# Projection of a windowless attention block: weights loaded once, the constant product earlier, more room for the attention's output

## The chip, the cores and the metric

One core of one Trainium2 chip runs the whole kernel. The metric is device time in microseconds, from one launch; the number quoted is the median over runs. The profile shows one execution of it. Units in the text are microseconds from the start of the profiled span unless another unit is named.

## The reference, cut to what matters

The input x is 2 images of 48 x 48 tokens with 768 channels, in float32. Layer 0 is attention over all 2304 tokens of an image, with 12 heads of 64 channels and a relative position term by row and by column; layer 1 mixes channels in the Fourier domain. What the change touches is the end of layer 0:

```python
x = x + attention(_gn(x))          # layer 0
    # attn = softmax(q k^T * scale + rel_h + rel_w)
    # out  = (attn @ v)  -> (B, 48, 48, 768)
    # return out @ proj_w + proj_b
x = x + fourier_mix(_gn(x))        # layer 1
```

`proj_w` is 768 x 768, which is 2.36 MB.

## The kernel before, in words

The two images run one after the other. For each, `attention` walks over 108 **units**: 6 pairs of heads, 6 groups g of 8 image rows, 3 parts x. Unit n is number 0 to 107 of an image. A unit has 128 queries, 2 heads and all 2304 keys, and goes through these steps:

- POOL writes the position terms of the unit into a tile `s` (`new_unit`, one 128 x 2304 operation for each head). There are three buffers of `s`.
- TensorE makes the scores by pieces of 512 keys (`ps_s`), DVE adds them to `s` and keeps the maxima (`mx`, then `nm`).
- ACT makes the exponentials in place (`numerators`).
- DVE transposes 32 x 32 blocks (`squares`, in two halves), and `exchange` moves the blocks between partitions into `pT`: 3 of 4 by DMAs from SP's queue, the fourth by ACT. When the second half has left, the buffer of `s` is free again.
- TensorE multiplies by the values (`weigh`, tile `ps_o`, two units later), ACT copies the result to `res`, and at each third unit SP sends it to `oT` in DRAM. The sums of exponentials are inverted, turned by TensorE (`ps_i`) and sent to `inv_d` in DRAM, for three groups at a time (`inverses`, with `turn` and `send`).

While a pair is weighed, the keys, values and queries of the next are made, so TensorE has work between the units. The last pair has no next one.

In the loop over n, one step is: scores of n, exponentials, work ahead, then what `late` fills in, then weighing of n - 2, then the second half of the exchange of n - 1, the first half of n, `finish`, the next `new_unit`, and the next step of `late`. Most instructions of `attention` and `Projection` are issued through `InOrder`, so that they keep the written order on their engine; others (`new_unit`, the bias addition, the loads of constants) may be put elsewhere by the scheduler. Line 68 is the helper that records all `InOrder` operations, so groups there are told apart by their tiles. A DMA from SP uses one of eight completion lanes in turn and waits for the one that used the lane before it.

`Projection` (line 571 on) lives in the large buffer `span`, which held the normalised input `xnT` during attention: the weights `w`, the bias `pb`, two buffers of a group of attention output `o_sb` (384 tokens, 768 channels) and one of the inverses `inv`, both read back from DRAM by `parts` and multiplied by POOL (`proj<-proj` in the profile). Its steps are run at the ends of units 102 to 108:

| unit | SP and POOL (`step`) |
|---|---|
| 102, 103, 104 | two sixths of `proj_w` each |
| 105 | half of group 0 of `oT`, `proj_b` |
| 106 | other half, first half of `inv` |
| 107 | second half of `inv`, POOL's multiplication |
| 108 | all of group 1 |

The bias of the values, times `proj_w`, is a constant row (`values_bias`, tile `ps_pb`): it is made once, in image 1, added to `pb` by DVE (line 638), and kept in DRAM as `pb_d` for image 2. `product(t, hf)` makes a 128-token, 384-channel piece of the projection (tile `acc`, 6 matmuls, 36 pieces in an image). `late(n - len(order) + 2)` puts some of this TensorE work in front of the last weighings: in image 1 half of the constant product before weighing 105, the other half and one piece before 106, three pieces before 107; in image 2 two pieces before 106 and three before 107.

`project_out` then loops over 18 tiles of 128 tokens: it loads rows of x into `x2` (`rows`), POOL adds `pb`, TensorE makes the remaining pieces, DVE adds each to its rows of `x2` (line 742), and finished rows go through the first Fourier matrix (`ps_y`, `over_w`) to DRAM. PSUM has seven rotating banks for all of this and one for `ps_o`.

Of the kernel before, what the change touches and what calls it, by code (L numbers as in the profile page):

```python
# [9 lines left out]
F32 = mybir.dt.float32  # L10
# [150 lines left out]


def attention(tc, k, x_b, a, oT, inv_d, late, span, ps_b, ps_o):

# [8 lines left out]
    with ExitStack() as ctx:  # L176
# [319 lines left out]
        for n in range(len(order) + 3):  # L496
            un = older = None
            if n < len(order):
                un = ahead
                pr, g, x = order[n]  # L500
                if g == 4 and x == 0 and pr + 1 < NP:
                    weights[0] = load_w(0, pr + 1)
                scores(un)
                recent.append(un)
            write = read = None
            if un is not None:
                numerators(un)
                ready, staged = staged, None
                if x == 2:
                    if n + 4 < len(order):  # L510
                        key = order[n + 4][:2]
                        staged = (key, queries(*key))
                    if g == 2 and pr + 1 < NP:
                        weights[2] = load_w(2, pr + 1)
                    if g == 5 and pr + 2 < NP:
                        weights[1] = load_w(1, pr + 2)
                elif n < 2:
                    for i in range(3):
                        values(0, 3 * n + i)
                    if n:  # L520
                        weights[1] = load_w(1, 1)
                elif pr + 1 < NP:
                    i = 2 * g + x
                    for j in range(0 if n == 3 else i, i + 1):
                        (keys if j < 6 else values)(pr + 1, j % 6)
                if ready is not None:
                    key, qT = ready
                    rhw, write, read = relative(key[1], qT)
                    groups[key] = (qT, rhw)
            if turn is not None:  # L530
                turn()
                turn = None
            if n >= len(order) - 1 and recent:
                late(n - len(order) + 2)
            if n > 1 and recent:
                older = recent.pop(0)
                weigh(older)
            evict(by_act)
            if last is not None:
                squares(last, 1)  # L540
                exchange(last, 1)
            if write is not None:
                write()
            if un is not None:
                squares(un, 0)
                exchange(un, 0)
            evict(by_dve)
            if read is not None:
                read()
            if older is not None:  # L550
                finish(older)
            if un is not None and n + 1 < len(order):
                ahead = new_unit(*order[n + 1])
            if send is not None:
                send()
                send = None
            if older is not None and older["x"] == 2 and older["g"] % 3 == 2:
                turn, send = inverses(older["pr"], older["g"] // 3)
            if len(order) - 6 <= n <= len(order):
                late()  # L560
            last = un


# [12 lines left out]
class Projection:  # L576


    def __init__(self, tc, k, a, oT, inv_d, span, ps_b, dram):
        self.nc = nc = tc.nc  # L580
        self.k, self.a, self.ps_b, self.dram = k, a, ps_b, dram
        self.oT_v = oT.rearrange("(cc p) s -> p cc s", p=P)
        self.inv_d = inv_d
        self.whole = span.tile([P, NCC * S], F32, tag="span", name="proj")
        self.w = self.whole[:, : NCC * C].rearrange("p (cc f) -> p cc f", f=C)
        self.pb = self.whole[:, NCC * C : (NCC + 1) * C]
        self.o = {}
        self.pe, self.sync, self.pool = (
            InOrder(tc, e) for e in (nc.tensor, nc.sync, nc.gpsimd)
        )  # L590
        w_v = a["proj_w"].rearrange("(cc p) f -> p cc f", p=P)
        load = lambda cc: nc.sync.dma_start(out=self.w[:, cc], in_=w_v[:, cc])
        parts = iter(self.parts(0))
        self.steps = [
            lambda: (load(0), load(1)),
            lambda: (load(2), load(3)),
            lambda: (load(4), load(5)),
            lambda: (next(parts), self.bias()),
            lambda: next(parts),
            lambda: list(parts),  # L600
            lambda: self.tokens(1),
        ]
        self.accs, self.waiting, self.late = {}, [], 1
        if k.pb_d is None:
            self.late = 0
            self.waiting += [lambda hf=hf: self.values_bias(hf) for hf in range(2)]
        for t in range(3):
            self.waiting += [lambda t=t, hf=hf: self.product(t, hf) for hf in range(2)]

    def step(self):  # L610
        self.steps.pop(0)()

    def fill(self, n):

        for _ in range(n - self.late):
            self.waiting.pop(0)()
        self.late = 0

    def bias(self):

# [3 lines left out]
    def values_bias(self, hf):  # L624


        nc, k = self.nc, self.k
        cols = slice(hf * UQ, (hf + 1) * UQ)
        ps = self.ps_b.tile([P, 512], F32, tag="b", name="ps_pb")
        for cc in range(NCC):  # L630
            self.pe.matmul(
                ps[:, :UQ],
                lhsT=k.bv[:, cc : cc + 1].to_broadcast([P, P]),
                rhs=self.w[:, cc, cols],
                start=(cc == 0),
                stop=(cc == NCC - 1),
            )
        nc.vector.tensor_tensor(self.pb[:, cols], ps[:, :UQ], self.pb[:, cols], ALU.add)
        if hf:
            k.pb_d = self.dram.tile([C], F32, tag="pb_d", name="pb_d")  # L640
            nc.sync.dma_start(out=k.pb_d, in_=self.pb[0, :])

    def product(self, t, hf):

        if (t, hf) not in self.accs:
            o_sb = self.o[t // 3]
            acc = self.ps_b.tile([P, 512], F32, tag="b", name="acc")
            for cc in range(NCC):
                self.pe.matmul(
                    acc[:, :UQ],  # L650
                    lhsT=o_sb[:, cc, (t % 3) * P : (t % 3 + 1) * P],
                    rhs=self.w[:, cc, hf * UQ : (hf + 1) * UQ],
                    start=(cc == 0),
                    stop=(cc == NCC - 1),
                )
            self.accs[t, hf] = acc
        return self.accs[t, hf]
# [5 lines left out]

    def parts(self, g):

        at = [(NCC + 1) * C + i * NCC * UQ for i in range(3)]
        o_sb, inv = (
            self.whole[:, c0 : c0 + NCC * UQ].rearrange("p (cc s) -> p cc s", s=UQ)
            for c0 in (at[g % 2], at[2])
        )  # L670
        for h in range(2):
            cc = slice(h * NCC // 2, (h + 1) * NCC // 2)
            self.sync.dma_start(out=o_sb[:, cc], in_=self.oT_v[:, cc, g * UQ : (g + 1) * UQ])
            if h == 0:
                yield
        for h in range(2):
            self.sync.dma_start(
                out=inv[h * HD : (h + 1) * HD],
                in_=self.inv_d[:, g // 3, h, g % 3, :].partition_broadcast(HD),
            )  # L680
            if h == 0:
                yield
        self.pool.tensor_tensor(o_sb, o_sb, inv, ALU.mult)
        self.o[g] = o_sb
        yield


def project_out(tc, k, x_b, pr, pools, y_d, x2, constants):
# [366 lines left out]
def block_kernel(tc, a, out):  # L1055
    nc = tc.nc
    B = a["x"].shape[0]
    with ExitStack() as ctx:
# [11 lines left out]
        nc.gpsimd.memset(k.eps, GN_EPS)  # L1070
        k.load(nc, a, cp, {"rel": [P, 2 * REL]})
        k.pb_d = None
        k.bv = cp.tile([P, NCC], F32, tag="bv", name="bv")
        with nc.allow_non_contiguous_dma(reason="biases onto partitions"):
            nc.sync.dma_start(
# [3 lines left out]
        for b in range(B):  # L1079
            oT = dram.tile([C, S], F32, tag=f"oT{b}", name=f"oT{b}")  # L1080
            y_d = dram.tile([YP, HW // 2, C], F32, tag=f"y_d{b}", name=f"y_d{b}")
            inv_d = dram.tile([NP, 2, 2, 3, UQ], F32, tag=f"inv_d{b}", name=f"inv_d{b}")
            ready = []

            def late(fill=0):
                if not ready:
                    ready.append(Projection(tc, k, a, oT, inv_d, span, ps_b, dram))
                if fill:
                    ready[0].fill(fill)
                else:  # L1090
                    ready[0].step()

            attention(tc, k, a["x"][b], a, oT, inv_d, late, span, ps_b, ps_o)
            with ExitStack() as ctx2:
                pool = lambda name, bufs, **kw: ctx2.enter_context(
# [9 lines left out]
                with ExitStack() as ctx3:  # L1105
                    work = ctx3.enter_context(tc.tile_pool(name="po_w", bufs=2))
                    project_out(
                        tc, k, a["x"][b], ready[0], (ps_b, work), y_d, x2, constants
                    )
                u_pool, w_pool, z_pool = pool("sp_u", 6), pool("sp_w", 2), pool("sp_z", 1)  # L1110
                y_pool = pool("sp_y", 8)
# [100 lines left out]
```

## Time and profile before

| | |
|---|---|
| median of 3 runs | 3811.16 us (3810.2 to 3815.46) |
| the profiled execution | 3818.63 us |
| its span, first to last instruction | 3816.8 us |
| mean granted TensorE clock | 0.978 |
| TensorE busy (PE) | 3660.0 us, 96% |
| DVE, ACT, POOL busy | 2845.0, 2516.4, 1993.1 us |
| DMA | 607.00 MB, 67.4% of 16 engines on SP's queue |
| handover from attention to projection, image 1 | about 1390 to 1500 us |
| the same, image 2 | about 3294 to 3400 us |

In a timeline, each row is the start, the duration, the engine, the line, the operation with output <- input, the shape, the count of instructions merged, and in brackets the idle time before it with what ended it. SPq rows are issues of DMAs, not their transfers. In a table of stretches a stretch is start:end, its length, and the busy time of PE, PEld, DVE, ACT and POOL with counts, then the granted clock, the DMA share and the rate. A float32 matmul is two rows for TensorE.

### The profile page before, as it was taken

The numbers are of one execution on the slowest core, as the hardware profiler recorded it, in microseconds if no ns is written. First come the engines' busy times: TensorE is split into PE (matmuls) and PEld (weight loads), VectorE is DVE, ScalarE is ACT, GpSimd is POOL, SyncE is SP. The second block draws the span as 40 slices with busy tenths as digits, with TensorE's granted clock in tenths as the row PEclk, the third lists the DMA queues.
The fourth block names the chain that finished last, engine by engine and source line by source line (L and its number), as shares of the span: only waits on it lengthen the run. The fifth ranks groups of instructions, "written<-read, shape, count | busy, mean of one in ns | idle before, by whom it ended". The sixth has DMA issues, their size and how long they took to land.

```text
span 3816.8 us, 83418 instructions
## 1 busy us (share of the span) xinstructions
PE 3660.0 (96%) x31520; PEld 2596.1 (68%) x31520; DVE 2845.0 (75%) x6692; ACT 2516.4 (66%) x3690; POOL 1993.1 (52%) x598
## 2 busy tenths in 40 slices
PE   8999999999999887999989999999999999879999
PEld 6677776767777665566666777777677776645665
DVE  4788888888888883335557988889888898833445
ACT  3688888888888882133237888888888888821331
POOL 2466666666666664412125666666666666633121
PEclk9999999999999998999989999999999999989899
DMA  3677777777777887633526777777777778885334
GB/s 103 144 176 167 174 170 170 173 163 178 166 176 166 171 190 184 165 101 110 167 81 143 172 173 168 177 165 174 164 177 166 173 171 170 194 189 151 103 103 134
DMA packets 497821, 607.00 MB, mean 159 GB/s; under 512 B 180493, under 2 KB 312973, under 8 KB 497422
## 3 DMA queue, kind: packets, MB, share of 16 engines
q1 hardware_dynamic: 497422, 601.69, 67.4%
q8 instruction: 250, 4.10, 0.5%
q14 instruction: 149, 1.22, 0.1%
HBM read 131.61 MB, written 87.67 MB: 57 GB/s over the span
## 4 chain that ended last, share of the span: by engine, by line
PE 84%; DMA 5%; DVE 4%; POOL 3%; SPq 2%; issue 1%; ACT 1%; POOLq 0%; DVEq 0%; ACTq 0%
PE ps_o L68 20%; PE ps_s L68 19%; PE ps_proj L68 14%; PE ps_v L68 8%; PE acc L68 7%; PE ps L948 4%; DVE s L68 3%; POOL s L344 3%; DMA pT<-s 2%; PE ps_z L892 2%; PE ps L920 2%; PE ps L924 2%; PE ps_u L983 2%; SPq L68 2%; PE ps_y L721 2%; PE ps_r L68 1%
## 5 line engine op out<-in xcount | busy, mean ns | idle before, releaser
L344 POOL TENSOR_TENSOR s<-rhw 128x2304 f32<-128x2304 f32 x432 | 1744.8, 4060 | 1144.6 <-DMA pT<-s 601.1
L68 DVE CUSTOM_DVE_ANT_0 s<-ps_s,s 128x512 f32<-128x512 f32 (+1 forms) x2160 | 1223.6, 633 | 371.7 <-issue 243.3
L68 ACT ACTIVATE s<-s,nm 128x1152 f32<-128x1152 f32 x864 | 1074.7, 1245 | 452.5 <-DVE nm L68 414.8
L68 DVE STREAM_TRANSPOSE s<-s 128x1152 f32<-128x1152 f32 x864 | 1111.8, 1344 | 5.5 <-ACT s L68 5.5
L68 ACT COPY pT<-s 32x1152 f32<-32x1152 f32 x864 | 993.2, 1150 | 19.5 <-DVE s L68 2.1
L68 PE MATMUL ps_o<-pT,v 128*64 128x128 f32 x15552 | 919.7, 278 | 47.9 <-DMA pT<-s 21.8
L68 PEld LDWEIGHTS ps_o<-pT,v 128*64 128x64 f32 x15552 | 867.8, 140 | 112.2 <-issue 53.8
L68 PE MATMUL ps_s<-kT,qT 64*128 64x512 f32 (+1 forms) x4320 | 918.5, 558 | 13.4 <-DVE mx L68 9.8
L68 PEld LDWEIGHTS ps_s<-kT,qT 64*128 64x128 f32 x4320 | 431.4, 186 | 450.7 <-issue 333.9
L68 PE MATMUL ps_proj<-xnT,w 128*128 128x384 f32 (+1 forms) x2016 | 597.0, 450 | 2.3 <-ACT gn_rstd L151 2.3
L68 PEld LDWEIGHTS ps_proj<-xnT,w 128*128 128x128 f32 x2016 | 360.8, 191 | 209.0 <-DVE mx L68 41.0
L68 PE MATMUL acc<-proj 128*128 128x384 f32 x864 | 287.5, 492 | 40.5 <-POOL proj L68 40.5
L742 DVE TENSOR_TENSOR x<-acc,x 32x384 f32<-32x384 f32 (+2 forms) x216 | 119.2, 553 | 277.3 <-PE acc L68 192.6
L68 PEld LDWEIGHTS ps_v<-w,xnT 128*128 128x128 f32 x2592 | 295.9, 193 | 21.2 <-DVE mx L68 21.2
L68 PE MATMUL ps_v<-w,xnT 128*128 128x128 f32 x2592 | 308.1, 279 | 0.0
L965 POOL TENSOR_TENSOR spectrum<-spectrum 128x480 f32<-128x480 f32 x80 | 96.3, 1204 | 345.0 <-DVE spectrum L964 186.6
L68 PEld LDWEIGHTS acc<-proj 128*128 128x128 f32 x864 | 165.8, 193 | 156.6 <-POOL proj L68 41.3
L728 ACT COPY y<-ps_y 112x384 f32<-112x384 f32 x96 | 45.9, 478 | 265.8 <-PE ps_y L721 248.7
L68 DVE DVE_READ_ACCUMULATOR2_ANT mx<- 128x1 f32 x2160 | 178.9, 83 | 0.0
L68 POOL TENSOR_TENSOR proj<-proj 128x2304 f32<-128x2304 f32 x12 | 60.6, 5052 | 197.5 <-DMA proj<-inv_d 169.7
L68 ACT ACTIVATION_READ_ACCUMULATOR s<-s,nm 128x1 f32 x864 | 161.1, 186 | 0.0
L928 ACT ACTIVATE spectrum<-ps,b 96x400 f32<-96x400 f32 x96 | 56.6, 589 | 147.7 <-PE ps L924 147.7
(97 smaller groups left out, 2099.6 us busy)
## 6 DMA issues: line engine op xcount, KB each, us to landing
pT<-s SPq DMA_DIRECT2D x2592, 144.0 KB
t<-rel SPq DMA_DIRECT2D x144, 189.0 KB
rhw<-t SPq DMA_DIRECT2D x144, 144.0 KB
y<-y_d SPq DMA_DIRECT2D x40, 360.0 KB
u_d<-spectrum SPq DMA_DIRECT2D x40, 360.0 KB
u<-u_d SPq DMA_DIRECT2D x48, 300.0 KB
xt<-in_x SPq DMA_DIRECT2D x12, 1152.0 KB
w<-in_qkv_w SPq DMA_DIRECT2D x36, 384.0 KB
```

What stands on the lines that cost most here:

```text
L68: return lambda *args, **kw: self.tc.keep_in_program_order(op(*args, **kw))
L344: nc.gpsimd.tensor_tensor(s[:, h, :].rearrange("p (y x) -> p y x", x=HW), rhw[:, x, h, :HW][:, :, None].to_broadcast([P, HW, HW]), rhw[:, ...
L721: nc.tensor.matmul(ps[:YP, : 2 * SC], lhsT=k.fw, rhs=part[:, t0 : t0 + 2, ch], start=True, stop=True,)
L728: nc.scalar.copy(y1[:, :, ch], ps[:YP, : 2 * SC].rearrange("p (t c) -> p t c", c=SC))
L742: nc.vector.tensor_tensor(dst, acc[p : p + n, :UQ], dst, ALU.add)
L892: nc.tensor.matmul(ps[:BS, w * 96 : (w + 1) * 96], lhsT=self.y2[s, j][:, w, i * BS : (i + 1) * BS], rhs=k.fh, start=True, stop=True,)
L920: nc.tensor.matmul(ps[:BS, :400], lhsT=w1[:, wa, i, :], rhs=zf[:, 0, fs], start=True, stop=False,)
L924: nc.tensor.matmul(ps[:BS, :400], lhsT=w1[:, wb, i, :], rhs=zf[:, 1, fs], start=False, stop=True,)
L928: nc.scalar.activation(self.o1[:, ri, fs], ps[:BS, :400], AF.Gelu, bias=self.b1[:, n, ri : ri + 1])
L948: nc.tensor.matmul(ps[64 * r : 64 * r + 64, w * BS : (w + 1) * BS], lhsT=self.o1[:, ri, f0 : f0 + 64], rhs=w2[:, (0, 2, 1, 0)[2 * r + ri], ...
L965: nc.gpsimd.tensor_tensor(val, val, clip, ALU.subtract)
L983: nc.tensor.matmul(ps[: 2 * HW, :480], lhsT=k.ih, rhs=d2[:, c0 : c0 + 480], start=True, stop=True)
```

## The change

- **Weights once.** `proj_w` gets a tile of its own (`k.w`, 18 KB in each partition) for the whole kernel, loaded by one DMA at the end of unit 3 of image 1 and used for both images.
- **Constant product in the last pair.** `values_bias` is filled in by the iterations of units 103 and 104 instead of 107 and 108.
- **Room.** The space that the weights leave in `span` is given to a third buffer of `o_sb` and a second one of `inv`.
- **Earlier first group.** The steps of group 0 run at units 102, 103 and 104, with the bias at 102; units 105 to 107 have empty steps; group 1 stays at 108. The products ahead are 1, 2 and 3 pieces before the weighings 105, 106 and 107, in both images.
- The closure `late` becomes the class `Late`, and a scratch size for dynamic DMAs is set to 1024.

```diff
-            if n >= len(order) - 1 and recent:
-                late(n - len(order) + 2)
+            if n >= len(order) - 6 and recent:
+                late.fill()
...
+            if n == 3:
+                late.weights()
             if len(order) - 6 <= n <= len(order):
-                late()
+                late.step()
...
-        self.w = self.whole[:, : NCC * C].rearrange("p (cc f) -> p cc f", f=C)
-        self.pb = self.whole[:, NCC * C : (NCC + 1) * C]
+        self.pb = self.whole[:, :C]
...
-        load = lambda cc: nc.sync.dma_start(out=self.w[:, cc], in_=w_v[:, cc])
-        parts = iter(self.parts(0))
+        parts = self.parts(0)
         self.steps = [
-            lambda: (load(0), load(1)),
-            lambda: (load(2), load(3)),
-            lambda: (load(4), load(5)),
             lambda: (next(parts), self.bias()),
             lambda: next(parts),
-            lambda: list(parts),
+            lambda: next(parts),
+            lambda: None,
+            lambda: None,
+            lambda: None,
             lambda: self.tokens(1),
         ]
...
+        bias = [lambda hf=hf: self.values_bias(hf) for hf in range(2)] if k.pb_d is None else []
+        early = [
+            lambda t=t, hf=hf: self.product(t, hf) for t in range(3) for hf in range(2)
+        ]
+        self.waiting = [[], bias[:1], bias[1:], [], [], early[:1], early[1:3], early[3:]]
...
-        at = [(NCC + 1) * C + i * NCC * UQ for i in range(3)]
+        at = [C + i * NCC * UQ for i in range(5)]
...
-            for c0 in (at[g % 2], at[2])
+            for c0 in (at[g % 3], at[3 + g % 2])
...
+class Late:
...
+    def weights(self):
+
+        if not self.k.w_there:
+            self.k.w_there = True
+            self.sync.dma_start(
+                out=self.k.w, in_=self.a["proj_w"].rearrange("(cc p) f -> p cc f", p=P)
+            )
...
+        k.w = cp.tile([P, NCC, C], F32, tag="w", name="w")
...
-    nc = bacc.Bacc("TRN2", target_bir_lowering=False, num_devices=1)
+    nc = bacc.Bacc("TRN2", target_bir_lowering=False, num_devices=1, dynamic_dma_scratch_size=1024)
```

More of the change, by code (lines that the diff above doesn't have):

```diff
@@ L590, in __init__, with fill @@
         )
-        w_v = a["proj_w"].rearrange("(cc p) f -> p cc f", p=P)
-        load = lambda cc: nc.sync.dma_start(out=self.w[:, cc], in_=w_v[:, cc])
-        parts = iter(self.parts(0))
+        parts = self.parts(0)
         self.steps = [
-            lambda: (load(0), load(1)),
-            lambda: (load(2), load(3)),
-            lambda: (load(4), load(5)),
             lambda: (next(parts), self.bias()),
             lambda: next(parts),
-            lambda: list(parts),
+            lambda: next(parts),
+            lambda: None,
+            lambda: None,
+            lambda: None,
             lambda: self.tokens(1),
         ]
[L603 to L608, printed above, removed]
+        bias = [lambda hf=hf: self.values_bias(hf) for hf in range(2)] if k.pb_d is None else []
[3 more added lines that the diff above has]
+        self.waiting = [[], bias[:1], bias[1:], [], [], early[:1], early[1:3], early[3:]]
+        self.accs = {}
     def step(self):
         self.steps.pop(0)()
[L613 to L617, printed above, removed]
+    def fill(self):
+        for issue in self.waiting.pop(0):
+            issue()
     def bias(self):
@@ L633, in values_bias @@
                 lhsT=k.bv[:, cc : cc + 1].to_broadcast([P, P]),
-                rhs=self.w[:, cc, cols],
+                rhs=k.w[:, cc, cols],
                 start=(cc == 0),
@@ L651, in product @@
                     lhsT=o_sb[:, cc, (t % 3) * P : (t % 3 + 1) * P],
[L652 removed]
+                    rhs=self.k.w[:, cc, hf * UQ : (hf + 1) * UQ],
                     start=(cc == 0),
@@ L685, in parts, with __init__, fill, step @@
         yield
+class Late:
+    def __init__(self, tc, k, a, *rest):
+        self.k, self.a, self.made = k, a, None
+        self.make = lambda: Projection(tc, k, a, *rest)
+        self.sync = InOrder(tc, tc.nc.sync)
+    def weights(self):
[4 more added lines that the diff above has]
+            )
+    def fill(self):
+        self.made = self.made or self.make()
+        self.made.fill()
+    def step(self):
+        self.made = self.made or self.make()
+        self.made.step()
 def project_out(tc, k, x_b, pr, pools, y_d, x2, constants):
@@ L1072, in block_kernel @@
         k.pb_d = None
+        k.w = cp.tile([P, NCC, C], F32, tag="w", name="w")
+        k.w_there = False
         k.bv = cp.tile([P, NCC], F32, tag="bv", name="bv")
@@ L1082, in block_kernel @@
             inv_d = dram.tile([NP, 2, 2, 3, UQ], F32, tag=f"inv_d{b}", name=f"inv_d{b}")
[L1083 to L1091, printed above, removed]
+            late = Late(tc, k, a, oT, inv_d, span, ps_b, dram)
             attention(tc, k, a["x"][b], a, oT, inv_d, late, span, ps_b, ps_o)
@@ L1107, in block_kernel @@
                     project_out(
-                        tc, k, a["x"][b], ready[0], (ps_b, work), y_d, x2, constants
+                        tc, k, a["x"][b], late.made, (ps_b, work), y_d, x2, constants
                     )
```

## The prediction

> **What bounds the kernel now.** I read the granted clock first (0.978 in the one profiled execution), then busy time by stretch, then engine by engine the timeline where attention hands over to the projection, because every edit acts there. Over most of attention TensorE is never idle (300.00 us busy of 300.00 between 600 and 900 us), so nothing there pays but less TensorE work, and the change has exactly as many matmuls as before. At the handover it is otherwise. By stretch (PE, PEld, DVE, ACT, POOL, then clock, DMA share, GB/s):
>
> ```profile
> 300.00:600.00 300.00, 300.00 (x2790) 217.23 (x2791) 264.91 (x631) 250.58 (x346) 192.08 (x48) 1.00 0.76 170
> 1390.00:1430.00 40.00, 31.69 (x286) 23.96 (x288) 31.50 (x75) 30.77 (x41) 24.00 (x7) 0.83 0.99 225
> 1430.00:1470.00 40.00, 21.39 (x183) 14.04 (x179) 22.36 (x49) 22.15 (x28) 12.12 (x3) 0.81 0.94 219
> ```
>
> The last six units of image 1 fill the DMA engines and leave TensorE idle for a quarter to half of the time. TensorE's timeline shows where the long gap is:
>
> ```profile
> 1433.56 3.70 PE L68 MATMUL ps_s<-kT,qT 64*128 64x512 f32 x14
> 1440.04 4.14 PE L68 MATMUL ps_pb<-proj,bv 128*128 128x384 f32 x12
> 1444.10 4.15 PE L68 MATMUL ps_o<-pT,v 128*64 128x128 f32 x72
> 1448.18 4.14 PE L68 MATMUL ps_pb<-proj,bv 128*128 128x384 f32 x12
> 1470.60 6.50 PE L68 MATMUL acc<-proj 128*128 128x384 f32 x12 [18.28 <-POOL proj L68]
> 1481.11 11.88 PE L68 MATMUL acc<-proj 128*128 128x384 f32 x36
> 1497.12 15.65 PE L68 MATMUL acc<-proj 128*128 128x384 f32 x48
> ```
>
> The last scores end at 1440.1 (T). The first product waits 18.28 us for POOL's multiplication of group 0. After 1497 TensorE runs without a gap to 1644: the projection is TensorE-bound. A product is 12 of these rows (each matmul is two) and takes 15.48/4 = 3.87 us at full clock. The queue, POOL and DVE rows that the steps need:
>
> ```profile
> 1393.49 1.01 SPq L592 DMA_DIRECT2D proj<-in_proj_w  x2
> 1471.91 0.61 SPq L68 DMA_DIRECT2D x<-in_x  x1
> 1497.41 0.35 SPq L68 DMA_DIRECT2D oT<-res  x1
> 1497.86 2.38 SPq L68 DMA_DIRECT2D inv_d<-turned  x3
> 1405.55 8.07 POOL L344 TENSOR_TENSOR s<-rhw 128x2304 f32<-128x2304 f32 x2 [8.13 <-DMA pT<-s]
> 1418.37 8.07 POOL L344 TENSOR_TENSOR s<-rhw 128x2304 f32<-128x2304 f32 x2 [4.75 <-DVE mx L68]
> 1429.56 8.08 POOL L344 TENSOR_TENSOR s<-rhw 128x2304 f32<-128x2304 f32 x2 [3.11 <-DMA pT<-s]
> 1465.51 5.03 POOL L68 TENSOR_TENSOR proj<-proj 128x2304 f32<-128x2304 f32 x1 [27.88 <-DMA pT<-s]
> 1390.95 5.15 DVE L68 STREAM_TRANSPOSE s<-s 128x1152 f32<-128x1152 f32 x4
> 1399.22 0.69 DVE L68 CUSTOM_DVE_ANT_0 s<-ps_s,s 128x512 f32<-128x512 f32 x1 [3.08 <-issue]
> ```
>
> **1. What is gained: the wait for group 0, and more products under attention.** Before, from T to TensorE's steady stretch: image 1, 1497.3 - 1440.1 = 57.2 us with 4 of 36 products done, 32 left; image 2 (scores end 3341.6, steady at 3399.8) 58.2 us with 31 left; there the same gap is 22.2 us. After, group 0 is multiplied before the last unit's scores, so TensorE runs from T on: 1 product, weighing 105, 2 products, weighing 106, 3 products, weighing 107: 6 x 3.87 + 3 x 4.1 = 35.5 us. Call its end W = T + 35.5. The exchange of unit 107 does not hold it: before, its last DMA was issued 22.7 us after T.
>
> **2. What is late next: the rows of x.** In the built order of the changed kernel, SP's `x<-in_x` no longer stands before `oT<-res` and the three `inv_d<-turned` of the last unit, but behind them. Before it was issued 25 us ahead of `oT<-res`; now it can only follow weighing 107: by the rows above, 0.34 us to `oT<-res`, 0.45 to the first and 2.4 for the three `inv_d`, so W + 3.3. Six accumulators hold six of seven PSUM banks until DVE adds them to rows of x. The seventh, freed when the small transpose of the inverses is copied, takes one more product (the first of group 1, which POOL has multiplied by about W: loads issued near T + 18, 13 us to land, 5.03), and then TensorE stops. Landing: between 6 and 21 us the 1.18 MB loads of x run at 398 to 411 GB/s, and the first, issued at 1.67, lets TensorE start at 8.21: 6.5 us; in image 2 before, the same load took 13.3 us (issued 3371.64, POOL starts on it at 3384.98), but behind 2.4 MB of group 1. Now the queue ahead is empty, so I take 6, with 5 and 13.3 as ends. Then two rows of POOL (1.8 us each) and DVE's adds (0.55): 4.3. TensorE resumes at W + 3.3 + 6 + 4.3 = W + 13.6; after the gap of 9 us it runs slowly (6.50 us for the first product after the 18 us gap, against 3.87), so I add 2: W + 15.6, with 29 products left.
>
> The Trainium skill (TensorE: Matmul & The Clock Gate, Part 1) says that an idle window of about 3.4 us halves TensorE's clock until about 3.4 us of work have passed. It speaks against trading one gap for another: by it the new gap would cost up to 1.7 us of lost work, against the 2 taken from the row. The trace agrees with the halving: the granted clock is 0.50 from 1456 to 1474.
>
> From T: 35.5 + 15.6 = 51.1 us. Image 1: 57.2 - 51.1 + 3 x 3.87 = **17.7** gained; image 2: 58.2 - 51.1 + 2 x 3.87 = **14.8**. Later groups do not wait: group 2's load is issued by about W + 10 and took 13.5 us before (1503.1 to 1516.6), and is needed near W + 40. The third buffer therefore gains nothing by itself; it was not waited for before (TensorE had no gap there).
>
> **3. What moves T: image 1.** `proj_b` is now loaded at unit 102, in the place of the first weights (1393.49), behind half of group 0 (0.59 MB). DVE's first addition of the constant product stands, in the built order, between unit 103's maxima (1390.87) and the transposes at 1390.95, and must wait for that load. Queued behind it on DVE are these transposes; for them wait the exchange DMAs, POOL (three buffers of s in a ring) and the next scores. Ahead of the load the reads of rhw land at 1398.8 (chain of waits), then 0.98 MB at 225 to 400 GB/s: about 1402.3. Ends: 1396 (the stall is then 5 us, of which 3 were idle anyway) and 1408 (13.3 us after issue, as the x row). So the transposes start near 1402.9, unit 104's scores at 1408 instead of 1399.2 (+9). Around the ring: POOL gets unit 102's buffer 7 us after its transposes end, at 1412.5 instead of 1405.55, unit 105's scores end 8.5 late, and unit 106's 7 late, since part is made up in the 4 to 8 us that POOL idled between tiles. Then comes POOL's multiplication of group 0 (5.03 us), which the built order puts between units 106 and 107: 1434 to 1439, unit 107's tile until 1447 instead of 1437.6. Unit 107's scores end near 1452 instead of 1443.1: T is **8.9** late. The 2.36 MB of weights that go from this stage don't relieve it at once: 2.75 MB of groups and bias are now in units 102 to 104 and not in 105 to 107. The constant product itself (2 x 4.14) fits into gaps of 2.9 and 3.5 us that TensorE had there: nothing, or 1 us each where it doesn't fit.
>
> **4. What moves T: image 2.** No constant product. Units 102 and 103 load 0.98 and 1.18 MB instead of 0.79 each, and of smaller pieces: at the 215 GB/s of group loads against 400 of weights, +1.7 and +3.5 us for the buffers that POOL waits for; unit 106's scores end 3.5 late. The multiplication then takes POOL from 3332.1 to 3337.2 and unit 107's tile ends at 3345.3 instead of 3338.8; the scores, 5.1 us of which need it, end at 3350.4 instead of 3344.5: T is **5.9** late. Ends of this: 2.9 (POOL's 5.03 less its 2.2 us idle) and 8.
>
> **5. The weights' single load.** 2.36 MB after unit 3's reads of rhw (149.85), where SP was idle until 153.78. At 405 GB/s it is 5.8 us, at 225 10.5. TensorE has no gap there, so a delay is lost: the next exchange lands 1.5 to 6 us late, against 1 us of margin at unit 6's scores. I take **1**, ends 0 and 5. The Fourier constants, now behind x, land by W + 10 and are first used near W + 20; the second layer's tables are first used 150 us later: nothing.
>
> **Sum.** 17.7 + 14.8 - 8.9 - 5.9 - 1 = 16.7 us gained. The profiled execution took 3818.63 us (span 3816.8 and 1.8 around it), 7.5 above the median of the runs, 3811.16. The same difference from the median gives **3794 us**; a profile would show a span near 3800.
>
> By the skill's page on DMA (DMA: Bandwidth & Descriptors, Anatomy of one DMA), a load takes 2 us and bytes at 436 GB/s: an estimate of 4.7 us for x against the 6 taken, and 7.4 us for the weights; with it the sum would be 2.6 us better.
>
> **Rivals.**
> *The stalls are hidden* (0.12). If `proj_b` lands by 1396, T in image 1 is late by POOL's multiplication alone, 3 us, and a sum of 22 to 26 remains: 3785 to 3789. For it: unit 104's scores had 3 us to spare. Against: a DMA share of 0.99 at that place.
> *Late landings, slower* (0.14). Every load that the change puts on the path lands as the slowest near row, 13.3 us after issue: x in both images (+14.6), the bias (+5.7 in image 1), group 0's divisors at POOL (+2): 16.7 - 22.3, so 3817. It decides from landings of about 11.5 us. For it: group loads took 13.5; against: the queue is empty at W. If only x is late, 3809, which is no change (0.12).
> *It doesn't do what it says*: excluded, since the built order has one load of the weights, at unit 3, and six products ahead.
>
> **How the numbers follow.** Forecast 0.62 (its own range 3783 to 3803). About 0.2%, or 7.6 us, is what a measurement of this kernel can tell from no change. Faster: forecast and hidden stalls, less a little, 0.72; same 0.14; slower 0.14. Range 3780 to 3813: hidden stalls with a quick x below, half of the slower rival above.
>
> **What would show it.** Right: no 18 us gap before the first product; a gap of about 9 us one product after weighing 107, ended by DVE's adds to x; DVE idle about 11 us before the addition in image 1 only; POOL's multiplication between units 106 and 107. Wrong: if x lands before W, if unit 107's scores end as early as before, or if units 4 to 7 of image 1 show TensorE gaps over 5 us.

## The result and the profile after

The changed kernel took **3810.81 us** (median of 12 runs, 3803.2 to 3817.08) beside 3812.27 us for the kernel before (12 runs); the ratio is 0.9994, 95% interval 0.9985 to 1.0003. A second group of runs gave 3812.57 us (11) beside 3816.48 us (27), again 0.9994 (0.9985 to 1.0002). So the change makes no difference that can be measured. The forecast was 16.7 us faster, so it was wrong, although 3811 lies inside the stated range.

Every event that the prediction named can be seen in the profile. First the stretches of the last six units (PE, PEld, DVE, ACT, POOL, clock, DMA share, GB/s):

```profile
1390.00:1430.00 40.00, 30.21 (x226) 19.47 (x226) 26.60 (x67) 23.54 (x31) 17.99 (x5) 0.85 0.79 185
1430.00:1470.00 40.00, 37.69 (x324) 26.58 (x322) 28.79 (x62) 30.91 (x41) 19.30 (x5) 0.94 0.83 174
```

The DMA share has fallen from 0.99 and 0.94, and the second stretch, which held the 18.28 us gap, is nearly full. But TensorE is no busier in the first (30.21 us against 31.69), and later comes a new gap. TensorE's timeline of image 1:

```profile
1403.32 1.27 PE L68 MATMUL ps_s<-kT,qT 64*128 64x512 f32 x2 [2.72 <-DVE proj L635]
1409.04 2.93 PE L68 MATMUL ps_s<-kT,qT 64*128 64x512 f32 x6 [4.44 <-DVE mx L68]
...
1451.40 4.11 PE L68 MATMUL acc<-w,proj 128*128 128x384 f32 x12
...
1488.10 4.11 PE L68 MATMUL acc<-w,proj 128*128 128x384 f32 x12 [0.39 <-issue]
1502.65 6.06 PE L68 MATMUL acc<-w,proj 128*128 128x384 f32 x12 [10.45 <-DVE x L764]
```

The products run ahead from T = 1451.4 without a wait for group 0. One product after weighing 107 TensorE stops for 10.45 us, and then the first product takes 6.06 us. The two gaps on top, in unit 104's scores, stand behind VectorE, whose addition to `proj_b` waits for the load of `proj_b` and holds up what is queued behind it. VectorE's, SyncE's and POOL's timelines at these places:

```profile
1402.71 0.56 DVE L635 TENSOR_TENSOR proj<-ps_pb,proj 128x384 f32<-128x384 f32 x1 [10.15 <-DMA proj<-in_proj_b]
```

```profile
1487.84 0.34 SPq L68 DMA_DIRECT2D oT<-res  x1
1488.27 2.37 SPq L68 DMA_DIRECT2D inv_d<-turned  x3
1490.69 0.45 SPq L68 DMA_DIRECT2D x<-in_x  x1
```

```profile
1436.19 5.08 POOL L68 TENSOR_TENSOR proj<-proj 128x2304 f32<-128x2304 f32 x1
1441.22 8.08 POOL L343 TENSOR_TENSOR s<-rhw 128x2304 f32<-128x2304 f32 x2
...
1498.45 14.14 POOL L68 TENSOR_TENSOR x<-x,proj 96x768 f32<-96x768 f32 x8 [11.41 <-DMA x<-in_x]
```

VectorE stood for 10.15 us before the addition. The rows of x are issued 3.26 us after weighing 107 (1487.43) and reach POOL 7.76 us later. Image 2 has the same gap, and there the first early product is slow too; POOL, SyncE and TensorE of image 2:

```profile
3386.48 0.45 SPq L68 DMA_DIRECT2D x<-in_x  x1
...
3394.41 14.15 POOL L68 TENSOR_TENSOR x<-x,proj 96x768 f32<-96x768 f32 x8 [13.94 <-DMA x<-in_x]
```

```profile
3344.55 6.71 PE L68 MATMUL acc<-w,proj 128*128 128x384 f32 x12
...
3398.62 6.98 PE L68 MATMUL acc<-w,proj 128*128 128x384 f32 x12 [10.66 <-DVE x L764]
```

A difference of a few us in the whole can't be read from one execution of each kernel: the spectral layer takes 253.6 to 259.3 us in image 1 (up to the norm of image 2) and 258.5 to 264.2 us in image 2 from one profile to the next, though none of the edits touches its lines. From R to Z the two profiles of the changed kernel agree within 1.3 us for each stage. So I read the account by stages of TensorE's timeline. u8: start of unit 8's scores; R: end of the last `ps_r`, a small product behind the position terms (in unit 102); T: end of the last scores; W: end of the last weighing (the start of the row behind it); Z: first `ps_z` of the spectral layer. The columns are times between these points in us.

```
                      image 1                              image 2
             0-u8    u8-R     R-T    T-W     W-Z      R-T    T-W     W-Z
before     206.05  1172.38   61.68  56.89  157.70    60.72  58.03  153.83
changed    210.07  1169.88   71.45  36.03  163.23    66.26  38.56  164.36
a_again    212.05  1169.98   70.45  35.98  163.81    65.03  37.72  163.94
e1         207.20  1169.95   70.79  36.03  163.23    66.66  38.60  164.40
e2         212.45  1171.15   65.74  36.03  163.76    65.48  37.73  163.90
e3         210.80  1170.33   70.55  35.98  151.10    65.42  36.04  151.06
e4         210.98  1170.02   70.84  40.72  162.80    64.68  41.01  164.26
e5         210.65  1169.99   58.48  55.73  157.72    58.18  60.25  153.84
e6         210.97  1171.11   71.67  38.13  164.53    61.01  38.50  163.79
e7         206.81  1171.70   66.59  37.28  151.09    65.36  37.47  151.06
e8         206.18  1170.30   65.99  37.72  151.10    62.18  37.62  151.07
e9         206.68  1173.99   70.53  36.04  164.52    64.98  36.03  163.79
```

By the mean of the changed kernel's two profiles against before: image 1 gains 15.1 us from T to Z and loses 9.3 before T; image 2 gains 9.6 and loses 4.9; the weights' load costs 4.4 (0-u8: mean 211.1 in the seven profiles with the load at unit 3, 206.7 in e1, e7, e8 and e9, which have it elsewhere). Sum 6.1 us gained, where 16.7 was forecast. The stage u8 to R, where the one profile of the kernel before is 2.4 us longer, is left out of this account: no step of the change acts there.

The cost of the weights' load is clearer when it is counted from the start of unit 3's scores, just ahead of the load, to u8: the five profiles without a load there (before, e1, e7, e8, e9) all take 61.96 or 61.97 us, the seven with it 65.00 to 67.31, which is 3.0 to 5.3 us more (mean 4.6).

### The profile page after: what moved, and what is told of

Its sections match the earlier page's. It is cut to its first block, busy times and chain, and to the rows that moved or that the text cites. A ratio compares the mean times of both kernels' runs of the same rounds, so it can differ in the third digit from the quotient of the medians.

```text
span 3807.0 us, 83396 instructions
## 1 busy us (share of the span) xinstructions
PE 3662.2 (96%) x31520; PEld 2592.2 (68%) x31520; DVE 2845.4 (75%) x6692; ACT 2517.0 (66%) x3690; POOL 1992.8 (52%) x598
## 4 chain that ended last, share of the span: by engine, by line
PE 86%; DMA 4%; POOL 3%; DVE 3%; SPq 1%; ACT 1%; issue 1%; POOLq 0%; DVEq 0%
PE ps_o L68 21%; PE ps_s L68 20%; PE ps_proj L68 14%; PE ps_v L68 8%; PE acc L68 7%; PE ps L970 4%; POOL s L343 3%; DVE s L68 2%; PE ps L942 2%; PE ps_u L1005 2%; PE ps_z L914 2%; PE ps L946 2%; PE ps_r L68 2%; PE ps_y L743 2%; SPq L68 1%; PE ps_x L1023 1%
## 5 line engine op out<-in xcount | busy, mean ns | idle before, releaser
L68 PE MATMUL acc<-w,proj 128*128 128x384 f32 x864 | 292.2, 497 | 21.9 <-DVE x L764 21.1
L68 PEld LDWEIGHTS acc<-w,proj 128*128 128x128 f32 x864 | 166.9, 194 | 141.1 <-DVE x L764 22.3
L970 PE MATMUL ps<-w,spectrum 96*64 96x96 f32 x3200 | 143.1, 248 | 0.0
```

The source lines that it names most:

```text
L68: return lambda *args, **kw: self.tc.keep_in_program_order(op(*args, **kw))
L970: nc.tensor.matmul(ps[64 * r : 64 * r + 64, w * BS : (w + 1) * BS], lhsT=self.o1[:, ri, f0 : f0 + 64], rhs=w2[:, (0, 2, 1, 0)[2 * r + ri], ...
```

## The experiments

My theory: separate costs on TensorE's path (the weights' load, `proj_b`, the wait for x, POOL's multiplication, the early loads of group 0), each of which can be taken away alone. The rival: the gains and losses shift into the next wait, so that single edits return nothing. All kernels below are the changed kernel with the edit shown.

**e1, weights loaded ahead of the unit loop.**

```diff
         for which in (0, 1):
             weights[which] = load_w(which, 0)
+        late.weights()
...
-            if n == 3:
-                late.weights()
```

> The changed kernel with one move: the projection's weights are loaded behind the first query and key weights, ahead of the unit loop, instead of at unit 3. Theory (the load held the exchanges of units 3 to 6): TensorE's gaps of 0.99 and 1.09 us around 166 and 175 us go, unit 8's scores start near 206 us again instead of 210.07, and the time falls by 4 to 5 us against the changed kernel, to about 3806. Rival (the delay at unit 3 is made up later, or the early load delays the first keys by as much): no difference over 1.5 us, 3811.

Measured: 3810.24 us, ratio to before 0.9986 (0.9977 to 0.9994). In the changed kernel TensorE had these gaps after unit 3:

```profile
166.49 4.15 PE L68 MATMUL ps_o<-pT,v 128*64 128x128 f32 x72 [0.99 <-DMA pT<-s]
175.37 1.31 PE L68 MATMUL ps_s<-kT,qT 64*128 64x256 f32 x4 [1.09 <-DVE mx L68]
```

Both are gone in e1, and unit 8 starts at 207.20, 4 us sooner than the mean with the load (211.1), as the theory has it. The medians alone can't tell 3 or 4 us from the changed kernel, since its own interval overlaps.

**e9, the same load at unit 30.** This tells whether unit 3 was a bad place.

```diff
-            if n == 3:
+            if n == 30:
                 late.weights()
```

> The changed kernel with the weights' load at unit 30 instead of unit 3. Theory (TensorE has no gap anywhere in attention and 2.36 MB hold the exchanges of two units wherever they are put): unit 8 starts near 206 us, 4 us sooner, but the stage from there to unit 103 takes 1174 us instead of 1170, and the time stays that of the changed kernel, near 3812. Rival (unit 3 is a tight place, because the second pair's keys and the ring of s buffers have only just filled; later the exchanges have slack): the stage stays at 1170 us, T comes 4 us earlier, and the time falls by 3 to 5 us, as with the early load.

Measured: 3810.56 us, ratio 0.9984 (0.9974 to 0.9993). Unit 8 starts at 206.68, but u8 to R takes 1173.99 us, 3.5 above the mean of the ten other profiles of changed kernels (1169.9 to 1171.7), with gaps of TensorE right behind the load, which was issued at 492.03. TensorE in e9:

```profile
506.32 4.15 PE L68 MATMUL ps_o<-pT,v 128*64 128x128 f32 x72 [1.72 <-ACT s L68]
515.25 1.31 PE L68 MATMUL ps_s<-kT,qT 64*128 64x256 f32 x4 [1.14 <-DVE mx L68]
516.48 4.29 PE L68 MATMUL ps_v<-w,xnT 128*128 128x128 f32 x36
```

The same `ps_v` row in the changed kernel:

```profile
516.08 4.29 PE L68 MATMUL ps_v<-w,xnT 128*128 128x128 f32 x36
```

From u8 to this row e9 takes 309.80 us and the changed kernel 306.01: 3.8 us are lost right at the load. (The stage alone would prove less, since the kernel before took 1172.38 us for it without a load there.)

So about 4 us are paid at both places where the load meets the exchanges; ahead of the unit loop it is free. The total is no judge of this: its interval holds both expected times.

**e2, the constant product one unit later.**

```diff
-        self.waiting = [[], bias[:1], bias[1:], [], [], early[:1], early[1:3], early[3:]]
+        self.waiting = [[], [], bias[:1], bias[1:], [], early[:1], early[1:3], early[3:]]
```

> The changed kernel with the constant product's two halves at units 104 and 105 instead of 103 and 104; the loads stay where they are. Theory (DVE's first addition waited 10.15 us for proj_b, and the ring of three s buffers passed that on): DVE's addition waits for TensorE only, and the last scores of image 1 (T) end 5 to 8 us earlier, 1445 instead of 1451.4 relative to the same start; time 3804 to 3806. Rival (the last six units of image 1 are held by the DMA queue itself, whose bytes are the same): T moves by less than 2 us and the time stays near 3811.

Measured: 3812.0 us, ratio 0.9989 (0.9981 to 0.9998). VectorE's first addition now waits for nothing of `proj_b`:

```profile
1410.21 0.56 DVE L635 TENSOR_TENSOR proj<-ps_pb,proj 128x384 f32<-128x384 f32 x1 [1.12 <-DMA pT<-s]
```

R to T falls from 70.95 (mean of the changed kernel's two profiles) to 65.74 us, by 5.2, at the lower end of the theory's 5 to 8; image 2, which has no such product, is unchanged. The median of these runs does not show it. What remains above before (61.68), 4 us, is not `proj_b`. POOL's timeline of e2 shows where it arises:

```profile
1426.09 8.08 POOL L343 TENSOR_TENSOR s<-rhw 128x2304 f32<-128x2304 f32 x2 [7.13 <-DMA pT<-s]
1434.13 5.07 POOL L68 TENSOR_TENSOR proj<-proj 128x2304 f32<-128x2304 f32 x1
1439.15 8.08 POOL L343 TENSOR_TENSOR s<-rhw 128x2304 f32<-128x2304 f32 x2
```

Counted from R, unit 106's tile starts 2.6 us later than before the change (42.49 against 39.94), behind a longer wait for an exchange (7.13 us against 4.75), and unit 107's 4.4 us later (55.55 against 51.13), with the multiplication of 5.07 us where POOL had idled 3.11.

**e3, the last results from ScalarE's queue.** The edit takes nothing away but moves `oT<-res` and the three `inv_d<-turned` of the last unit off SyncE, so that x no longer stands behind them.

```diff
-                sync.dma_start(
+                (act if (pr, g) == (NP - 1, HW // 8 - 1) else sync).dma_start(
                     out=oT[...]
...
-                    sync.dma_start(
+                    (act if (pr, half) == (NP - 1, 1) else sync).dma_start(
                         out=dst[x],
```

> The changed kernel, in which the last unit's result (oT<-res) and its three inverses (inv_d<-turned) are issued from ScalarE's queue instead of SyncE's, so that the first rows of x stand right behind group 1's loads. Theory (TensorE's gap of about 10.5 us one product after weighing 107 is the wait for x behind the last results): x is issued 8 to 12 us sooner, the gap falls below 3 us in both images, and the time falls by 18 to 24 us against the changed kernel, to 3787 to 3793. Rival (x lands no sooner because it then shares the DMA engines with group 1, or the next wait, for group 2 or for POOL's additions, takes the gap's place): less than 6 us, 3805 to 3811.

Measured: **3781.9 us**, ratio 0.9915 (0.9902 to 0.9928). SyncE's queue and TensorE of image 1:

```profile
1474.73 0.36 SPq L68 DMA_DIRECT2D x<-in_x  x1
```

```profile
1488.83 7.98 PE L68 MATMUL acc<-w,proj 128*128 128x384 f32 x24 [0.89 <-POOL proj L68]
```

x is issued 16 us sooner (I had written 8 to 12). POOL, which multiplies group 1 until then, goes on to it without a wait, and the gap shrinks to 0.89 us:

```profile
1483.25 5.07 POOL L68 TENSOR_TENSOR proj<-proj 128x2304 f32<-128x2304 f32 x1 [34.11 <-DMA proj<-inv_d]
1488.28 7.10 POOL L68 TENSOR_TENSOR x<-x,proj 96x768 f32<-96x768 f32 x4
```

W to Z falls by 12.4 and 13.1 us. It is 151.1 in both images; before, less the two products or one that are now done ahead, it was 157.70 - 2 x 3.87 = 149.96 and 153.83 - 3.87 = 149.96. So but for about 1 us nothing takes the gap's place. The gain, some 30 us by the two ratios to before (0.9915 and 0.9994), is above the 24 that I expected; these stages give 25.5 of it, and the rest lies within what the other stages scatter from profile to profile.

**e4, POOL's multiplication of group 0 behind unit 107's tile.**

```diff
             lambda: next(parts),
             lambda: None,
-            lambda: None,
+            lambda: next(parts),
             lambda: None,
...
+        yield
         self.pool.tensor_tensor(o_sb, o_sb, inv, ALU.mult)
```

> The changed kernel with POOL's multiplication of group 0 behind the preparation of unit 107 instead of ahead of it; the loads stay. Theory (POOL's 5.07 us lie on the path of the last unit's scores): T of image 2 comes 3 to 5 us earlier, T of image 1 0 to 5 us (there the wait for proj_b is also on the ring), and the time falls by 4 to 9 us, to 3802 to 3807. Rival (the exchange DMAs, not POOL, hold the last unit's buffer; or the first product now waits for the later multiplication): 0 to 1 us, or 2 us slower.

Measured: 3821.61 us, ratio 1.0014 (1.0005 to 1.0023): slower than both kernels. The theory falls, and of the rival's two branches the later multiplication, for which the first product now waits, shows. POOL's and TensorE's timelines of image 1:

```profile
1441.65 8.08 POOL L343 TENSOR_TENSOR s<-rhw 128x2304 f32<-128x2304 f32 x2 [4.79 <-DVE mx L68]
1449.69 5.07 POOL L68 TENSOR_TENSOR proj<-proj 128x2304 f32<-128x2304 f32 x1
```

```profile
1454.81 5.83 PE L68 MATMUL acc<-w,proj 128*128 128x384 f32 x12 [2.98 <-POOL proj L68]
```

Unit 107's tile starts at 1441.65, 60.65 us after R, against 61.27 in the changed kernel: where the multiplication had been, POOL now idles 4.79 us. So in image 1, with the wait for `proj_b` still in place, the 5.08 us ran in what is otherwise an idle slot and cost T nothing (70.84 against 70.95). In image 2 it cost at most about 1 us (64.68 against 65.65), which is within the scatter of a stage; there too POOL idles where the multiplication had been:

```profile
3336.89 8.08 POOL L343 TENSOR_TENSOR s<-rhw 128x2304 f32<-128x2304 f32 x2 [3.71 <-DMA pT<-s]
```

Moved back, it holds the first product: T to W is 4.7 and 2.9 us longer.

**e5, the weights alone.** Group 0, `proj_b` and the constant product go back to their old units; the weights stay on chip.

```diff
         self.steps = [
-            lambda: (next(parts), self.bias()),
-            lambda: next(parts),
-            lambda: next(parts),
             lambda: None,
             lambda: None,
             lambda: None,
+            lambda: (next(parts), self.bias()),
+            lambda: next(parts),
+            lambda: next(parts),
...
-        self.waiting = [[], bias[:1], bias[1:], [], [], early[:1], early[1:3], early[3:]]
+        todo = bias + early
+        first = len(bias) // 2
+        self.waiting = [[], [], [], [], [], todo[:first], todo[first : first + 2], todo[first + 2 : first + 5]]
```

> The changed kernel with one part alone: the weights stay on chip (loaded at unit 3) and there are three group buffers, but group 0, proj_b and the constant product are put back to the units that they had before the change, and one or two products run ahead as before. Theory (the early group moves bytes into units 102 to 104, the weights alone only take bytes away): against the kernel before, 4 to 5 us are lost at unit 3, T comes 2 to 6 us earlier in each image, the 18 and 22 us gaps before the first product stay above 12 us; sum between 7 us faster and 1 us slower than before. The rows of x stand ahead of the last results again. Rival (the freed bytes do nothing, because the exchanges wait for SyncE's issue or for VectorE): T as before the change, and the time 4 to 5 us above the kernel before.

Measured: 3813.51 us, ratio 0.9994 (0.9985 to 1.0003). With 2.36 MB gone from each handover, T comes 3.2 and 2.5 us earlier than before the change; 4.6 us are lost at unit 3, and T to W is 2.2 us longer in image 2. The gaps before the first product stay, at 16.82 and 25.09 us. The weights on chip alone give nothing that can be measured: what they gain at the handover they cost at unit 3. That they are what lets the products start early is argued from the order of the loads; no run starts them early without the weights on chip.

**e6, group 0's loads spread over units 102 to 105**, one of the four in each.

```diff
             lambda: next(parts),
             lambda: next(parts),
-            lambda: None,
+            lambda: (next(parts), next(parts)),
             lambda: None,
             lambda: None,
...
             self.sync.dma_start(out=o_sb[:, cc], in_=...)
-            if h == 0:
-                yield
+            yield
...
                 in_=self.inv_d[...].partition_broadcast(HD),
             )
-            if h == 0:
-                yield
+            yield
```

> The changed kernel with group 0's four loads spread over units 102 to 105, one for each unit, and POOL's multiplication at unit 105; the built order still has it between units 106 and 107. Theory (after the run with the late multiplication: the heavier loads of units 102 and 103, not POOL, make T of image 2 late): the stage to T in image 2 falls from 66 to 62 to 64 us, in image 1 by at most 2 us (proj_b's wait stays), and the time by 3 to 6 us against the changed kernel. Rival (the bytes of the six units as a whole count, not their place): less than 1 us.

Measured: 3812.06 us, ratio 0.9990 (0.9981 to 0.9999). The expectation is wrong in one point: the multiplication came behind unit 107's tile, so this run holds e4's edit as well. TensorE's first product of image 1:

```profile
1455.83 4.14 PE L68 MATMUL acc<-w,proj 128*128 128x384 f32 x12 [2.08 <-POOL proj L68]
```

Image 2's R to T falls from 65.65 to 61.01. As e4 reached 64.68 with the multiplication alone, 3.7 us belong to the place of the loads. In image 1 R to T does not fall (71.67 against 70.95), though the loads are spread and the multiplication is late: there the wait for `proj_b` is still in place. The first product of image 1 waits as in e4, and T to W loses 2.1. The total doesn't move beside the changed kernel of the same group (3812.57).

**e7: the edits of e1, e2 and e3 together**, with no other line changed.

> Three edits of the changed kernel together: weights loaded ahead of the unit loop, constant product at units 104 and 105, the last results issued from ScalarE's queue. Theory (three separate places on TensorE's path, so they add): 29 us from x, 4 from the weights and 5 from proj_b, 35 to 39 us below the changed kernel run beside it, about 3774. Rival (the gains at unit 3 and at proj_b are given back before the end of the projection, as the medians of the single edits suggested): 28 to 31 us, about 3782.

Measured: **3774.26 us**, 38.3 below the changed kernel run beside it (3812.57); ratio to before 0.9888 (0.9873 to 0.9903). The stages show each gain again: 4.3 us to u8, 4.4 from R to T of image 1, 12.4 and 13.1 from W to Z, 34.2 in all; against it, T to W of image 1 is 1.3 longer. So the edits add, as the theory has it; what the total shows beyond the stages is not located.

**e8: e7, and one load of group 0 for each unit in image 2 alone.**

```diff
-        parts = self.parts(0)
+        parts, second = self.parts(0), k.pb_d is not None
...
-            lambda: next(parts),
+            lambda: [next(parts) for _ in range(1 if second else 2)],
             lambda: next(parts),
-            lambda: None,
+            lambda: second and next(parts),
...
             self.sync.dma_start(out=o_sb[:, cc], in_=...)
-            if h == 0:
-                yield
+            yield
```

> The three edits together (weights ahead of the unit loop, constant product one unit later, last results from ScalarE's queue), and in image 2 alone group 0's four loads spread over units 102 to 105, with POOL's multiplication behind the tile of unit 107. Theory (heavy loads in units 102 and 103 hold the exchanges of image 2): the stage to T in image 2 takes 61 us instead of 65, the first product then waits 2 to 3 us for POOL's multiplication, and the time lies 2 to 4 us below the three edits, 3770 to 3773. Rival (what T gains, the first product's wait takes back): 3774, as the three edits.

Measured: **3772.84 us**, ratio 0.9877 (0.9862 to 0.9893). R to T of image 2 is 3.2 us shorter than in e7, and T to W the same, with a wait of 1.57 us for POOL's multiplication where 2 to 3 were expected; the totals of e7 and e8 can't be told apart. Both are some 1% faster than either kernel.

**a_again, the changed kernel once more.**

> The changed kernel once more, unchanged, as the base for the others of this group. Expected 3808 to 3815 us; in its profile the stage from the last read-out of unit 103 to the last scores takes 71 us in image 1 and 66 us in image 2 again, and the gap before TensorE's second product of group 1 is 10 to 11 us in both images. If these stages scatter by more than 2 us between two profiles of the same kernel, the differences of single stages named so far mean little.

Measured: 3812.57 us; R to T 70.45 and 65.03 us, the gaps 10.72 and 10.67. The stages repeat well enough for the readings above; single differences below 1.5 us mean little.

## Why the prediction was wrong

The gains and losses were where the prediction put them. What failed are sizes: in step 2 the landing of x (6 us taken, 7.76 and 7.93 measured) and the slow product behind it, in step 1 the early products of image 2 (35.5 us taken, 38.56 and 37.72 measured), and in step 5 the weights' load (1 us taken, 4.4 measured). The net was a small difference of large terms, and these errors all went the same way.

**Step 2, x (the dearest miss).** Issue at W + 3.3: measured 3.26 and 3.30. POOL's and DVE's 4.3: 4.20 and 4.21. The **landing** was taken as 6 us and was 7.76 and 7.93; over the seven profiles in which x stands behind the last results it is 7.63 to 8.07 us. I had argued from an empty queue and from the first load of the execution. Here the small constants, a second load of x and group 2 followed it at once; whether they held it was not tried, so why it took longer stays open. Slow clock, 2: the first product took 6.06 and 6.98 us instead of 4.11, so 2.0 and 2.9. The granted clock across the gap, the first product and what follows:

```profile
1492.30:1502.60 10.30, 0.00 (x0) 0.00 (x0) 1.58 (x4) 0.00 (x0) 4.15 (x3) 0.70 1.04 238
1502.60:1508.50 5.90, 5.85 (x12) 3.31 (x13) 5.71 (x11) 0.00 (x0) 5.90 (x4) 0.66 1.09 280
1508.50:1515.00 6.50, 6.50 (x21) 3.71 (x20) 4.73 (x9) 1.92 (x4) 4.21 (x4) 1.00 1.09 219
```

The clock is back at 1.00 after that one product. The Trainium skill's formula for one DMA (DMA: Bandwidth & Descriptors, Anatomy of one DMA), which gave an estimate of 4.7 us for this load, is further off than the 6; it would have made the forecast still faster. The page fits it to DMAs that GpSimd issues, and these come from SyncE.

**Step 1, 35.5 us from T to W.** 36.0 in image 1, but 38.56 and 37.72 in image 2: there the first early product ran 6.71 us, at a granted clock of 0.61 after TensorE's gaps in units 106 and 107. It is not so in each execution (36.04 in e3 and 36.03 in e9). I had priced all six products at full clock. With the misses of step 2 the gains from T to Z are 15.1 and 9.6 instead of 17.7 and 14.8.

**Step 3, T of image 1, 8.9.** Measured 9.3, so the term was right, but not its parts, and the agreement is partly luck. Without the wait for `proj_b` T comes 5.2 us earlier (e2); 4 us remain. With that wait in place, neither the multiplication (e4) nor the place of the loads (e6) moves T: the wait hides them. In e2, without it, both are on POOL's path, 2.6 us of delay from an exchange and then the multiplication in place of an idle 3.11 us. I had 7 us from `proj_b` and added the multiplication to it; but in e4, with no multiplication ahead of it, unit 107's tile already starts 9.5 us later than before the change (60.65 us after R against 51.13). How the 4 us divide is not shown: no run takes loads or multiplication away in image 1 without the wait for `proj_b`.

**Step 4, T of image 2, 5.9.** Measured 4.9: loads 3.7 (e6 against e4) and multiplication 1.0. I had 3 and 2.9 for them: from the multiplication I had subtracted 2.2 us of POOL's idle time before unit 107's tile, but with the multiplication moved away POOL idled 3.71 us there, waiting for an exchange. The 1.0 is within the scatter, so it may be nothing.

**Step 5, the weights, 1 with ends 0 and 5.** Measured 4.4 by u8 (4.6 counted from unit 3), 3.8 by e9. The sentence "TensorE has no gap there, so a delay is lost" was right, and the value taken went against it: it set a margin, seen at one unit, against the delay of one exchange.

In sum, against the forecast: 2.6 (T to Z, image 1), 5.2 (image 2), 0.4 (step 3), -1.0 (step 4) and 3.4 (step 5) make 10.6, which leaves 6.1 of 16.7. The medians show 1.5 and 3.9. The 2 to 5 us between stay open: the kernel before was profiled once, and the stages that no edit touches scatter by more than that.

**The rivals.** "Stalls hidden" fails on the 10.15 us before the addition. "Late landings" named the right direction, and its mild case (only x late, no change) nearly the measured time, but with a landing of 13.3 us that didn't occur: 1.8 and 1.9 us for x, with the other terms above, came to the same, which is luck. The third group buffer was not tried by itself. Before, SyncE's later group loads waited for TensorE, 20.2 us in all in image 1, and with the third buffer they no longer do; but TensorE waits for no group's buffer in either kernel.

## What to carry to other kernels

When the forecast is a difference of gains and losses of nearly equal size, the error of each term counts in full, and most of the errors may go one way, as here: then "no change" deserves a large share of the chances. An edit that starts work early moves the next wait onto what is fetched behind that work: look in the built order for the load that now stands behind the last result, and move the stores of that result to another engine's queue; here moving four small DMA issues was worth 25.5 us by the stages and 29 by the medians, more than the 16.7 forecast for the whole change. Put a large load where the engine that sets the time isn't fed by DMA: here it was free ahead of the loop, and inside it cost about 4 us at both places tried.

## What the runs showed of the hardware

A single load of 2.36 MB cost about 4 us in a stretch where TensorE has no gap, although the DMA share without it is only 0.63 (before, 144 to 180 us) or 0.76 (changed kernel, 480 to 500 us), and nothing later made up for it (u8 to R takes 1169.88 us in the changed kernel and 1169.95 in e1). A load of 1.18 MB, issued by SyncE behind four small stores, took 7.63 to 8.07 us until POOL could start on it (fourteen cases in seven profiles), against 6.5 until TensorE could at the start of the execution.
